# A transformer block with a mixture of experts: how token rows are scattered to their experts, when the expert stage begins, and which queue writes the output

## The chip, the core and the metric

The kernel runs on one core of a Trainium2 chip. A core has TensorE (PE, the matrix multiplier), VectorE (DVE), ScalarE (ACT), GpSimd (POOL), and SyncE (SP), which only issues transfers (DMAs). POOL and ACT can issue DMAs too, each on a queue of its own. [...] PSUM holds what PE writes, in eight banks; SBUF is the on-chip memory; DRAM is the memory outside.

The metric is the device time of one execution in microseconds (us). Before the change it is 938.62 us, the median of three runs (936.95 to 940.47).

## The reference

Input x is 8 sequences of 512 tokens of 256 values. A layer norm feeds two branches whose results are added to x:

```python
xn = layernorm(x)
# attention: 16 heads of 64, causal, keys and values through a latent of 128
latent = xn @ w_kv_down
k, v   = split(latent @ w_kv_up);  q = xn @ w_q
att    = softmax(causal(q @ k.T / 8))
attn   = (att @ v) @ w_out
# feed-forward: 8 experts of width 128, two for each token, and a shared one of width 256
scores = sigmoid(xn @ gate_w.T + lb_bias);  topw, topi = top_k(scores, 2)
topw   = topw / (topw.sum(-1) + 1e-8)
for e in range(8):
    m = topi == e
    wmean = (topw * m).sum() / max(m.sum(), 1)
    y = (silu(xn @ gw[e].T) * (xn @ uw[e].T)) @ dw[e].T
    out += where(m.any(-1), y * wmean, 0)
out += shared_mlp(xn)
return x + attn + out
```

There are 4096 tokens, so 8192 pairs of a token and one of its experts. How many go to one expert depends on the data.

## The kernel before

**Experts by sorted rows.** The kernel does not multiply every token by every expert. A DRAM buffer `xg_d` has 39 tiles of 256 slots (`NET`, line 88: 8192 / 256 plus seven for the experts' last, partly filled tiles). The router (line 309) works out a slot for each token and choice, with each expert starting at a tile boundary. `scatter_rows(n)` (line 442) writes the 128 normalised rows of token tile n to their slots by two indirect DMAs on POOL's queue, one for each choice, with a small memset after each. A row has 256 values and 16 more; one of these is the token's number. 39 x 256 slots less 8192 rows leaves 1792 slots empty. Before the scatters, `fill_zeros` (line 238, 13 calls) writes the whole buffer with rows of zeros that carry the number of a spare row.

For each tile t of the 39, `expert_fetch` gathers the expert's weights (POOL's queue) and loads the 256 rows (SP's queue); `expert_turn` transposes the rows on PE; `expert_hidden` and `expert_down` are the two layers; and `expert_add` adds the results, 128 rows at a time, to the token's row in `acc_d`, the DRAM accumulator (an indirect, adding DMA on POOL's queue; each waits for the one before to have landed). `acc_d` is started with x by `begin_sums` (SP), and each sequence's projected attention and shared result is added to it by `add_projection` (POOL). At the end `bring_out` copies seven sequences from `acc_d` to the output, DRAM to DRAM; the eighth goes by way of SBUF.

**Attention by pairs.** The loop over m (line 902) runs over 64 pairs of heads: pair m is heads 2p and 2p+1 of sequence b, m = 8b + p. In each pair PE makes scores, four strips of 128 queries (line 619); VectorE adds the mask and finds minima (626); ScalarE takes the exponentials (633); VectorE transposes blocks of 32 x 32 into `blk` (646); sixteen DMAs of 80 KB carry the blocks into their places, `pt<-blk` (`moved`, 658, called the moves here); and two pairs later PE multiplies by the values (`weighted`, 708). ScalarE copies that out and POOL multiplies it by the inverse sums (721), which come by way of DRAM (`row`, on POOL's queue, and `rb`, on SP's). `blk` and `pt` have two buffers each.

**The order of the work** is written out by hand. `put(m, place, f)` puts a piece of work into pair m at a place; the loop takes it in order of place, between scores and exponentials. The engines' order follows the order of the calls. Three stages differ:

- pairs 0 to 13: layer norms of the next sequences, layout of the experts' weights, zero fills, and in pairs 11 to 13 the router (mostly VectorE). Up to here POOL issues 5 of a pair's 16 moves, SP 11.
- pairs 14 to 21 (`S0` = 14 to `E0` = `BLOCK0` = 22): the scatters, four token tiles a pair, eight indirect DMAs on POOL's queue. `scattering` gives POOL 1 of the 16 moves, ScalarE 5 (issued by `rest`, after the exponentials of the pair's first half) and SP 10. Until `BLOCK0` a pair's strips go in two groups, (0, 3) and (1, 2), and the values' product comes late in the pair.
- pairs 22 to 63: all strips in one group, (3, 1, 2, 0), the product earlier in the pair, and the 39 experts spread evenly over half-pairs: expert t stands at half-pair `first + t * n_halves // NET` = 49 + 67 t // 39, its fetch four half-pairs ahead. From pair 59 (`END`) POOL and SP issue eight moves each.

Output projections of a sequence (lines 802 to 806) fall in the third and fourth pair of the sequence after it, so in pairs 10, 11, 18, 19, 26, 27 and so on; shared hidden chunks in the fifth and sixth. These pairs are long on PE; those with neither are short.

Of the kernel before, what the change touches and what calls it, by code (L numbers as in the profile page):

```python
# [33 lines left out]
F32 = mybir.dt.float32  # L34
I32 = mybir.dt.int32
AF = mybir.ActivationFunctionType
ALU = mybir.AluOpType
AX = mybir.AxisListType
# [3 lines left out]
P = 128  # L42
MASKED = 1.0e30
NO_MIN = 3.0e38
TOPK = 2
SLOTS = 256
# [3 lines left out]
def kernel(  # L50
# [17 lines left out]
    nc = tc.nc  # L68

    B, T, C = x.shape  # L70
# [6 lines left out]
    E = gate_w.shape[2]  # L77
    I = eg_w.shape[3]
    NS = sd_w.shape[1]
    NT = B * T  # L80
    NTILE = NT // P
    NQ = T // P
# [4 lines left out]
    QSCALE = -(float(D) ** -0.5)  # L87
    NET = NT * TOPK // SLOTS + E - 1
    NU = SLOTS // P

    const = ctx.enter_context(tc.tile_pool(name="const", bufs=1))
    wts = ctx.enter_context(tc.tile_pool(name="wts", bufs=1))
    keep = ctx.enter_context(tc.tile_pool(name="keep", bufs=1))
# [28 lines left out]
    outf = out.rearrange("b t c -> (b t) c")  # L122
# [10 lines left out]
    W = C + 16  # L133
    xnp, tmp_pools = ExitStack(), ExitStack()
    xns = xnp.enter_context(tc.tile_pool(name="xnp", bufs=1)).tile([P, NTILE, W], F32, name="xn")
# [3 lines left out]
    def load_x(b, first=0, count=NQ, by=nc.sync):  # L139
# [40 lines left out]
        out=mask[:, T - P :],  # L180
# [52 lines left out]
            wall_d[:, ds(at, n)].rearrange("(e p) i -> p e i", p=P)[:, es], w  # L233
        )

    NZ = 3

    def fill_zeros(k):
        nc.gpsimd.dma_start(
            xg_d[ts(k, NZ * SLOTS), :].rearrange("(n p) c -> p n c", p=P),  # L240
            zero.unsqueeze(1).broadcast_to([P, NZ * NU, W]),
        )

    def begin_sums(b):

        if b == B:
# [62 lines left out]
    def router():  # L309
# [67 lines left out]
        nc.vector.tensor_reduce(tiles, need, AX.X, ALU.add)  # L377
        end = rt.tile([P, E], F32, name="end")
        nc.vector.tensor_tensor_scan(end, ones[:, :E], tiles, 0.0, ALU.mult, ALU.add)
        yield  # L380

        upto = rt.tile([P, E, NTILE], F32, name="upto")
# [52 lines left out]

    between = keep.tile([P, 1], F32, name="between")
    at_i = keep.tile([P, TOPK, NTILE], I32, name="at_i")
    wrow_i = keep.tile([P, NET], I32, name="wrow_i")
    coef = keep.tile([P, NET], F32, name="coef")


    def scatter_rows(n):

        for k in range(TOPK):
            ins = nc.gpsimd.indirect_dma_start(  # L445
                out=xg_d[:, :],
                out_offset=bass.IndirectOffsetOnAxis(ap=at_i[:, k, n : n + 1], axis=0),
                in_=xns[:, n, :],
                in_offset=None,
            )  # L450
            tc.declare_no_dep(ins.ins, group="scatter", reason="rows of different slots")
            tc.add_to_no_dep_group("scatter", ins.ins)
            nc.gpsimd.memset(between, 0.0)

    def swiglu(g, u, th, h):

# [20 lines left out]

    def expert_fetch(t):

        w = ep.tile([P, WR], F32, bufs=4, name="w")  # L480
        nc.gpsimd.indirect_dma_start(
            out=w[:, :],
            out_offset=None,
            in_=wall_d[:, :],
            in_offset=bass.IndirectOffsetOnAxis(ap=wrow_i[:, t : t + 1], axis=0),
        )
        xg = ep.tile([P, NU, W], F32, bufs=3, name="xg")
        nc.sync.dma_start(xg, xg_d[ts(t, SLOTS), :].rearrange("(u p) c -> p u c", p=P))
        fetched[t] = w, xg

    def expert_turn(t):
        xg = fetched[t][1]

        pss = [bank([P, NU, NCC, D], "ps_x") for _ in range(2)]
        for u in range(NU):
            for cc in range(NCC):
                for j in range(2):
                    nc.tensor.transpose(  # L498
                        pss[j][:, u, cc, :], xg[ts(j, D), u, ts(cc, P)],
                        ident[ts(j, D), ts(j, D)],  # L500
                    )
        xgT = ep.tile([P, NCC, SLOTS], F32, bufs=2, name="xgT")
        for j in range(2):
            nc.scalar.copy(
                xgT.rearrange("p c (u j q) -> p j u c q", j=2, q=D)[:, j], pss[j]
            )
        to = ep.tile([P, NU], I32, bufs=4, name="to")
        nc.gpsimd.tensor_copy(to, xg[:, :, C].bitcast(I32))
        turned[t] = xgT, to

# [242 lines left out]
        )  # L753

    def bring_out(b):
        nc.sync.dma_start(outf[ts(b, T), :], acc_d[ts(b, T), :])

    def bring_back():
        nc.sync.dma_start(
# [6 lines left out]

    EARLY, HALF = 0.3, 0.65
    S0 = 14
    E0 = BLOCK0 = S0 + NTILE // NQ
    plan: dict = {}  # L770

    def put(m, place, f, *a):
        if place >= 2:
            m, place = m + 1, place - 2
        plan.setdefault(m, []).append((place, len(plan[m]) if m in plan else 0, f, a))
# [57 lines left out]
    def put_half(h, place, f, *a):  # L833
        put(h // 2, h % 2 + place, f, *a)
# [16 lines left out]
    LN_END = ((B - 2) * LNH // 2 + 6) // 2  # L851
    for k in range(4 * NCC + 2):
        put(1 + k, 0.45, lay_out_weights, k)
    for k in range(NET // NZ):
        put(k, 1.45, fill_zeros, k)
    for b in range(B + 1):
        put(NPAIR + 1 if b == 0 else E0 - B + b - 1, 0.55, begin_sums, b)

# [11 lines left out]
    for k in range(12):  # L870
        put(R0 + k // 4, 0.35 + 0.5 * (k % 4), lambda: next(steps, None))
    assert S0 == R0 + 3
    for n in range(NTILE):
        put(S0 + n // NQ, 0.35 + 0.5 * (n % NQ), scatter_rows, n)


    def begin_experts():
# [8 lines left out]
    first, n_halves = 2 * E0 + 5, 2 * (END - E0) - 7  # L886
    for t in range(NET):
        h = first + t * n_halves // NET
        put_half(h - 4, 0.5, expert_fetch, t)
        put(h // 2, -1, expert_turn, t)  # L890
        put(h // 2, (0.23, 0.67)[h % 2], expert_hidden, t)
        put_half(h + 1, 0.15, expert_down, t)
        for u in range(NU):
            put_half(h + 2 + u, 0.45, expert_add, t, u)
# [125 lines left out]
```

## Time and profile before

| what | value |
|---|---|
| median of three runs | 938.62 us |
| profiled execution, whole | 948.27 us |
| its span | 946.5 us |
| PE busy | 902.4 us (95%) |
| POOL busy | 598.9 us (63%) |
| VectorE busy | 579.8 us (61%) |
| ScalarE busy | 506.3 us (53%) |
| granted clock of PE, mean | 0.984 |
| DMA, all | 190.76 MB, mean 202 GB/s |
| scatters `xg_d<-xn,at_i` | 64, 979 ns each on POOL |
| zero fills `xg_d<-zero` | 13 of 816 KB, 920 ns each on POOL |
| additions `acc_d<-ye,to` | 78, 1635 ns each on POOL |

The profile is of one execution, and lists for each group of instructions its line, engine, operation and tiles ("out<-in"), its busy time, and the idle time before it with what ended that idle time. "SPq", "ACTq" and "POOLq" are the issues of transfers by these engines. Stages can be cut out and the engines' busy time summed for each, with the granted clock of PE (1.00 is full) and the mean busy share of the 16 DMA engines. A DMA's issue takes its engine's time, and its data land later.

### The profile page before, as it was taken

The numbers are of one execution on the slowest core, as the hardware profiler recorded it, in microseconds if no ns is written. First come the engines' busy times: TensorE is split into PE (matmuls) and PEld (weight loads), VectorE is DVE, ScalarE is ACT, GpSimd is POOL, SyncE is SP. The second block draws the span as 40 slices with busy tenths as digits, with TensorE's granted clock in tenths as the row PEclk, the third lists the DMA queues.
The fourth block names the chain that finished last, engine by engine and source line by source line (L and its number), as shares of the span: only waits on it lengthen the run. The fifth ranks groups of instructions, "written<-read, shape, count | busy, mean of one in ns | idle before, by whom it ended". The sixth has DMA issues, their size and how long they took to land. (4 is left out here: it accounts for less than half of the span.)

```text
span 946.5 us, 20282 instructions
## 1 busy us (share of the span) xinstructions
PE 902.4 (95%) x6380; PEld 475.8 (50%) x6380; DVE 579.8 (61%) x2041; ACT 506.3 (53%) x1506; POOL 598.9 (63%) x825
## 2 busy tenths in 40 slices
PE   8898999998789889999999999999999999999998
PEld 3354455533344345554555545565555654555546
DVE  3975764895534667446665466744677446674671
ACT  3654654445444467545665456744577445674550
POOL 2795883427776865647766666685668666766560
PEclk9999999999899989999999999999999999999999
DMA  7589888667886988768888778887778978886892
GB/s 275 155 256 261 263 247 295 154 165 222 219 232 172 255 224 220 181 150 202 193 205 190 167 180 195 214 185 185 165 194 188 211 180 189 192 184 149 203 271 76
DMA packets 127225, 190.76 MB, mean 202 GB/s; under 512 B 24688, under 2 KB 88432, under 8 KB 126880
## 3 DMA queue, kind: packets, MB, share of 16 engines
q1 hardware_dynamic: 87984, 107.73, 42.0%
q0 software_dynamic: 36656, 78.19, 34.9%
q10 hardware_dynamic: 2480, 3.55, 1.5%
q8 instruction: 52, 0.85, 0.4%
q14 instruction: 53, 0.43, 0.2%
HBM read 66.45 MB, written 50.05 MB: 123 GB/s over the span
## 5 line engine op out<-in xcount | busy, mean ns | idle before, releaser
L626 DVE CUSTOM_DVE_ANT_0 ps_s<-ps_s,mask 128x128 f32<-128x128 f32 (+3 forms) x512 | 238.9, 519 | 200.3 <-PE ps_s L619 160.1
L633 ACT ACTIVATE pr<-ps_s,mn 128x128 f32<-128x128 f32 (+3 forms) x512 | 268.3, 535 | 131.7 <-DVE mn L626 89.0
L646 DVE STREAM_TRANSPOSE blk<-pr 128x384 f32<-128x384 f32 (+2 forms) x512 | 206.5, 445 | 25.7 <-DMA pt<-blk 6.0
L540 POOL DMA_INDIRECT acc_d<-ye,to x78 | 127.5, 1635 | 116.7 <-DMA acc_d<-ye,to 44.2
L665 POOL DMA_DIRECT2D pt<-blk x303 | 164.9, 720 | 46.3 <-PE ps_q L117 15.6
L619 PE MATMUL ps_s<-k,q 64*128 64x128 f32 (+3 forms) x1024 | 168.8, 448 | 12.0 <-issue 5.7
L708 PE MATMUL ps_y<-pt,v 128*64 128x512 f32 (+3 forms) x1024 | 159.7, 456 | 11.8 <-DMA xnT_d<-lnT 3.9
L619 PEld LDWEIGHTS ps_s<-k,q 64*128 64x128 f32 x1024 | 92.0, 188 | 73.3 <-issue 38.8
L721 POOL TENSOR_TENSOR yT<-yT,rb 128x512 f32<-128x512 f32 x62 | 85.9, 1385 | 67.6 <-ACT yT L720 56.3
L117 PE MATMUL ps_o<-wo_sb,yT 128*64 128x256 f32 x1024 | 121.5, 379 | 2.7 <-issue 2.7
L117 PE MATMUL ps_q<-xnT,wq_sb 128*64 128x512 f32 x512 | 121.9, 597 | 0.0
L708 PEld LDWEIGHTS ps_y<-pt,v 128*64 128x64 f32 x1024 | 74.6, 142 | 93.8 <-issue 72.9
L633 ACT ACTIVATION_READ_ACCUMULATOR pr<-ps_s,mn 128x1 f32 x512 | 108.0, 211 | 0.0
L117 PEld LDWEIGHTS ps_o<-wo_sb,yT 128*64 128x64 f32 x1024 | 77.4, 137 | 37.4 <-issue 5.3
L117 PE MATMUL ps_e<-xgT,w 128*64 128x256 f32 x624 | 74.1, 379 | 0.8 <-DMA w<-wall_d,wrow_i 0.8
L626 DVE DVE_READ_ACCUMULATOR2_ANT mn<- 128x1 f32 x512 | 72.4, 141 | 0.0
L117 PEld LDWEIGHTS ps_q<-xnT,wq_sb 128*64 128x64 f32 x512 | 37.7, 139 | 67.6 <-issue 61.9
L117 PE MATMUL ps_v<-wkv_sb,lat 128*64 128x256 f32 x512 | 68.2, 387 | 2.9 <-ACT k L584 2.9
L445 POOL DMA_INDIRECT xg_d<-xn,at_i x64 | 62.7, 979 | 13.2 <-issue 13.2
L117 PE MATMUL ps_k<-lat,wkv_sb 128*64 128x512 f32 x256 | 69.4, 620 | 1.0 <-issue 1.0
L687 POOL DMA_DIRECT2D row<-riT x64 | 50.9, 796 | 17.0 <-DVE riT L685 14.4
L744 ACT COPY po<-ps_o 128x256 f32<-128x256 f32 x28 | 10.5, 374 | 95.3 <-PE ps_o L117 80.0
(131 smaller groups left out, 955.3 us busy)
## 6 DMA issues: line engine op xcount, KB each, us to landing
pt<-blk SPq DMA_DIRECT2D x681, 80.0 KB
pt<-blk POOLq DMA_DIRECT2D x303, 80.0 KB
rb<-row SPq DMA_DIRECT2D x128, 128.0 KB
xg_d<-zero POOLq DMA_DIRECT2D x13, 816.0 KB
xg<-xg_d SPq DMA_DIRECT2D x39, 272.0 KB
acc_d<-in_x_dram SPq DMA_DIRECT2D x8, 512.0 KB
xin<-in_x_dram SPq DMA_DIRECT2D x7, 512.0 KB
xnT_d<-lnT SPq DMA_DIRECT2D x7, 512.0 KB
```

What stands on the lines that cost most here:

```text
L117: nc.tensor.matmul(out[ts(j, D)], lhsT[:, ts(j, D)], rhs, start=start, stop=stop)
L445: ins = nc.gpsimd.indirect_dma_start(out=xg_d[:, :], out_offset=bass.IndirectOffsetOnAxis(ap=at_i[:, k, n : n + 1], axis=0), in_=xns[:, n, :],
L540: nc.gpsimd.indirect_dma_start(out=acc_d[:, :], out_offset=bass.IndirectOffsetOnAxis(ap=turned[t][1][:, u : u + 1], axis=0), in_=results[t ...
L619: nc.tensor.matmul(pss[j][:, ds(at, n)], q[ts(j, D), ts(i, P)], k[ts(j, D), :n], start=True, stop=True,)
L626: nc.vector.tensor_tensor_reduce(out=pss[j][:, ds(at, n)], in0=pss[j][:, ds(at, n)], in1=mask[:, T - n :], scale=1.0, scalar=NO_MIN, op0=A ...
L633: nc.scalar.activation(o, s, AF.Exp, bias=mn, scale=-1.0, accum_out=rs[:, j, i : i + 1])
L646: nc.vector.transpose(blk[:, :, j, i : i + (nr - 1) * (NQ - 1) + 1 : NQ - 1, :].rearrange("p b c q -> p c b q"), pr[:, j, : nr * P].rearra ...
L665: by.dma_start(pt[ts(kb, QB), a], blks[b, p][ts(a, QB), kb])
L687: nc.gpsimd.dma_start(row.rearrange("a x q -> (a x) q"), riT)
L708: nc.tensor.matmul(ps[ts(j, D), :, c:, :], vs[b, h // VH][:, c, ts(h % VH, D)], pts[b, p][:, :, j, at : at + NQ - c, :], start=(c == 0), s ...
L721: nc.gpsimd.tensor_tensor(y, y, rb, ALU.mult)
L744: nc.scalar.copy(pos[b][:, tt % 2, :], ps)
```

## The change

- **Scatters.** Three token tiles a pair in place of four (`SR` = 3), so the 32 tiles take eleven pairs, 14 to 24. `E0` and `BLOCK0` become 25: strips in two groups, POOL's single move and ScalarE's five last until pair 24, and the 39 experts are spread over the half-pairs from 55 on: 55 + 61 t // 39. `begin_sums` for sequences 1 to 7 and the spare rows, which counts back from `E0`, moves three pairs later.
- **Zeros.** The 13 fills of the whole buffer go. The router finds the 1792 empty slots (eight more VectorE instructions in the step that ends with `end`), and 14 indirect DMAs on POOL's queue scatter 128 rows of zeros each to them (`scatter_empty`): seven in pair 13, and one in each of pairs 14 to 20. `scatter` is the part of `scatter_rows` that both use.
- **Fetches** stand five half-pairs ahead of their expert, not four, with a buffer more for the weights (5), the rows (4) and the token numbers (5).
- **Outputs.** `bring_out` issues its copies from ScalarE's queue, not SP's.

```diff
+    NEMPTY = (NET * SLOTS - NT * TOPK) // P
...
-    NZ = 3
-
-    def fill_zeros(k):
-        nc.gpsimd.dma_start(
-            xg_d[ts(k, NZ * SLOTS), :].rearrange("(n p) c -> p n c", p=P),
-            zero.unsqueeze(1).broadcast_to([P, NZ * NU, W]),
-        )
...
+        none = rt.tile([P, E], F32, name="none")
+        nc.vector.scalar_tensor_tensor(
+            none, tiles, float(SLOTS), cnt, ALU.mult, ALU.subtract
+        )
+        ahead = rt.tile([P, E], F32, name="ahead")
+        nc.vector.tensor_tensor_scan(ahead, ones[:, :E], none, 0.0, ALU.mult, ALU.add)
+        nc.vector.tensor_tensor(ahead, ahead, none, ALU.subtract)
+        kth = rt.tile([P, NEMPTY], F32, name="kth")
+        nc.vector.tensor_scalar(kth, count[:, :NEMPTY], float(P), here, ALU.mult, ALU.add)
+        past = rt.tile([P, NEMPTY, E], F32, name="past")
+        nc.vector.tensor_tensor(
+            past, kth.unsqueeze(2).broadcast_to([P, NEMPTY, E]),
+            ahead.unsqueeze(1).broadcast_to([P, NEMPTY, E]), ALU.is_ge,
+        )
+        nc.vector.tensor_tensor(
+            past, past, cnt.unsqueeze(1).broadcast_to([P, NEMPTY, E]), ALU.mult
+        )
+        filled = rt.tile([P, NEMPTY], F32, name="filled")
+        nc.vector.tensor_reduce(filled, past, AX.X, ALU.add)
+        nc.vector.tensor_tensor(empty_i, kth, filled, ALU.add)
...
     def scatter_rows(n):
         for k in range(TOPK):
-            ins = nc.gpsimd.indirect_dma_start(
-            ...
-            nc.gpsimd.memset(between, 0.0)
+            scatter(at_i[:, k, n : n + 1], xns[:, n, :])
+
+    def scatter(at, rows):
+        ins = nc.gpsimd.indirect_dma_start(
+            out=xg_d[:, :],
+            out_offset=bass.IndirectOffsetOnAxis(ap=at, axis=0),
+            in_=rows,
+            in_offset=None,
+        )
+        tc.declare_no_dep(ins.ins, group="scatter", reason="rows of different slots")
+        tc.add_to_no_dep_group("scatter", ins.ins)
+        nc.gpsimd.memset(between, 0.0)
+
+    def scatter_empty(k):
+        scatter(empty_i[:, k : k + 1], zero)
...
-        w = ep.tile([P, WR], F32, bufs=4, name="w")
+        w = ep.tile([P, WR], F32, bufs=5, name="w")
...
-        xg = ep.tile([P, NU, W], F32, bufs=3, name="xg")
+        xg = ep.tile([P, NU, W], F32, bufs=4, name="xg")
...
-        to = ep.tile([P, NU], I32, bufs=4, name="to")
+        to = ep.tile([P, NU], I32, bufs=5, name="to")
...
     def bring_out(b):
-        nc.sync.dma_start(outf[ts(b, T), :], acc_d[ts(b, T), :])
+        nc.scalar.dma_start(outf[ts(b, T), :], acc_d[ts(b, T), :])
...
     S0 = 14
-    E0 = BLOCK0 = S0 + NTILE // NQ
+    SR = 3
+    E0 = BLOCK0 = S0 - (-NTILE // SR)
...
-    for k in range(NET // NZ):
-        put(k, 1.45, fill_zeros, k)
...
+    for k in range(NEMPTY):
+        n = NEMPTY // 2
+        put(S0 - 1 + max(k - n + 1, 0), 0.37 + (k < n) * 0.2 * k, scatter_empty, k)
     for n in range(NTILE):
-        put(S0 + n // NQ, 0.35 + 0.5 * (n % NQ), scatter_rows, n)
+        put(S0 + n // SR, 0.35 + (0, 0.5, 1)[n % SR], scatter_rows, n)
...
-        put_half(h - 4, 0.5, expert_fetch, t)
+        put_half(h - 5, 0.5, expert_fetch, t)
```

More of the change, by code (lines that the diff above doesn't have):

```diff
@@ L437 @@
     at_i = keep.tile([P, TOPK, NTILE], I32, name="at_i")
+    empty_i = keep.tile([P, NEMPTY], I32, name="empty_i")
     wrow_i = keep.tile([P, NET], I32, name="wrow_i")
@@ L444, in scatter_rows @@
         for k in range(TOPK):
[L445 to L452, printed above, removed]
-            nc.gpsimd.memset(between, 0.0)
+            scatter(at_i[:, k, n : n + 1], xns[:, n, :])
[11 more added lines that the diff above has]
+        scatter(empty_i[:, k : k + 1], zero)
     def swiglu(g, u, th, h):
```

## The prediction

> **What bounds the kernel now.** I read the busy shares first: TensorE (PE) is busy 902.4 of 946.5 us, the next engine 598.9. So the time is PE's work plus PE's stalls, and I looked for where the stalls lie. The timeline of PE near the end gives the price of an undisturbed pair. Columns: start, us, then the instruction; a bracket is idle time before it and what ended it.
>
> ```profile
> 888.78 2.43 PE L619 MATMUL ps_s<-k,q 64*128 64x512 f32 x16
> 891.14 2.38 PE L708 MATMUL ps_y<-pt,v 128*64 128x512 f32 x16
> ...
> 897.06 2.43 PE L619 MATMUL ps_s<-k,q 64*128 64x512 f32 x16
> ...
> 905.33 2.43 PE L619 MATMUL ps_s<-k,q 64*128 64x512 f32 x16
> 909.86 4.07 PE L708 MATMUL ps_y<-pt,v 128*64 128x512 f32 x16 [2.10 <-DMA out_dram<-acc_d]
> ```
>
> From one set of scores to the next an attention pair alone takes 897.06 - 888.78 = 8.28 us. By the same timeline a latent adds 1.7, a shared hidden chunk 3.4, half an output projection 8.6, a turn of normalised rows 0.6, the logits 1.9. What a pair takes beyond its own sum is stall. Next, the busy time of each engine in stages cut at the pairs' starts (PE, PEld, DVE, ACT, POOL, then granted clock, DMA share, GB/s):
>
> ```profile
> 71.80:142.00 70.20, 63.69 (x382) 32.51 (x380) 45.02 (x170) 38.49 (x113) 52.41 (x67) 0.95 0.89 257
> ...
> 204.50:218.10 13.60, 11.47 (x62) 4.66 (x60) 13.39 (x50) 6.22 (x20) 3.79 (x6) 1.00 0.34 82
> 218.10:261.50 43.40, 33.89 (x158) 13.95 (x156) 22.44 (x86) 21.67 (x69) 35.19 (x61) 0.88 0.85 239
> ...
> 283.00:324.10 41.10, 41.10 (x270) 18.92 (x268) 24.03 (x85) 18.22 (x55) 30.04 (x49) 1.00 0.74 205
> 324.10:352.10 28.00, 22.48 (x121) 10.52 (x121) 18.60 (x66) 16.46 (x51) 20.09 (x34) 0.88 0.81 222
> 352.10:880.50 528.40, 523.26 (x4079) 289.61 (x4075) 319.31 (x1102) 305.37 (x907) 345.35 (x423) 1.00 0.81 188
> ```
>
> The expert stage (last line, pairs 24 to 59) idles 5.1 us in 528: PE sets it. The stalls are before it: pairs 5 to 9 (first line), pair 14 (VectorE full: 13.39 of 13.60), pairs 15 to 17 (third), pairs 22 and 23 (fifth). Pairs 19 to 21 scatter too, yet PE is full there, because projection and shared work cover the scatters. In pairs 15 to 17 PE's timeline starts at
>
> ```profile
> 229.80 0.68 PE L619 MATMUL ps_s<-k,q 64*128 64x128 f32 x4
> ...
> 245.19 0.49 PE L619 MATMUL ps_s<-k,q 64*128 64x128 f32 x4
> ...
> 257.18 4.40 PE L708 MATMUL ps_y<-pt,v 128*64 128x512 f32 x16
> 261.52 1.35 PE L619 MATMUL ps_s<-k,q 64*128 64x128 f32 x8
> ```
>
> so pairs 16 and 17 take 15.4 and 16.3 us for 8.28 of work (pair 15: 218.10 to 229.80, 11.7). Two queues are full there. POOL's timeline runs one cycle of eight scatters in 13.5 us, 227.75 to 241.27, with a scatter every 1.3:
>
> ```profile
> 227.75 0.57 POOL L665 DMA_DIRECT2D pt<-blk  x1
> ...
> 229.21 1.01 POOL L445 DMA_INDIRECT xg_d<-xn,at_i  x1 [0.30 <-issue]
> ...
> 230.53 0.99 POOL L445 DMA_INDIRECT xg_d<-xn,at_i  x1 [0.19 <-issue]
> ...
> 241.27 0.56 POOL L665 DMA_DIRECT2D pt<-blk  x1 [0.76 <-issue]
> ```
>
> And ScalarE stops its exponentials to issue its own moves (three here, five a pair):
>
> ```profile
> 230.39 1.90 ACTq L665 DMA_DIRECT2D pt<-blk  x3
> 232.34 0.47 ACT L633 ACTIVATE pr<-ps_s,mn 128x256 f32<-128x256 f32 x1 [2.39 <-DMA pt<-blk]
> ```
>
> Last, SP's timeline: eleven moves cost 12.52 us of issue in pair 4-5, 7.22 late in the expert stage; two output copies cost 2.19.
>
> ```profile
> 69.54 12.52 SPq L665 DMA_DIRECT2D pt<-blk  x11
> ...
> 847.48 7.22 SPq L665 DMA_DIRECT2D pt<-blk  x11
> ...
> 895.23 2.19 SPq L756 DMA_DIRECT2D out_dram<-acc_d  x2
> ```
>
> **The change, part by part.** I sum against the profiled execution (948.27, span 946.5) and put the difference on the median of 938.62; the profiled run is 1% longer than the median, which on a difference of ten is 0.1 us.
>
> A. *Zero fills gone.* Thirteen DMAs of 816 KB, 10.6 MB, leave POOL's queue, with 13 x 0.92 = 12.0 us of POOL. Six fall in 71.8 to 142: 4.9 of 70.2 x 257 = 18.0 MB, 27%. The DMA share of 0.89 would fall to some 0.65, below the 0.81 at which eleven moves take 7.22 to issue. Stalls beyond their own sums: pair 5, 20.71 us against 8.28 + 3.4 + 1.3 + 1.9 = 14.9, so 5.8; pair 8, 14.99 against 11.5, so 3.5; pair 6, 0.8. Both large ones end when late pt moves land. Bounds: 0 (the delay is the order on SP's queue) to -10. I take -6, nearest to the bandwidth row. In its place 14 scatters of 128 rows x 1088 B = 1.9 MB; seven go in pair 13, where POOL is idle 5.89 us before one instruction and 5.36 before the next: 7 x 1.3 = 9.1 fits. Without that cover 9.1 us would delay pair 14's move, which has a whole pair before it is read.
>
> B. *Finding the empty slots.* Eight more VectorE instructions in pair 12. Rows: five small ones like L391 (171 ns), three like L372 and L377 (291 and 286): 1.7 us. VectorE is full by pair 14, so I put +1.5 on the path (0 to 1.7).
>
> C. *Three tiles a pair over eleven pairs.* Pairs 14 to 20 carry seven scatters, 21 to 23 six, 24 four. The cycle of 13.5 becomes 12.2, 10.9 and 8.3. (i) Pairs 15 to 17 last 43.4 now; one scatter less should give 1.3 each, and pair 18, 4.6 over its sum from the lag, some 1. Here a rule weighs in. The last PE line but one above shows 16 matmuls in 4.40 us against 2.38: PE ran at half clock, 0.88 granted on the mean, though no idle gap here is over 2.5 us. The Trainium skill ("TensorE: Matmul & The Clock Gate", Part 1) has the clock fall after an idle window of about 3.4 us; by it these stalls would cost only their idle, 9.5 us. The row has 43.4 - 3 x 8.28 = 18.6. By the rule (i) is worth half, -2.5; by the row -5. I take the row (0 to -9). (ii) Pairs 22 to 24 become scatter pairs with two groups, and the experts' PE work they held moves later, unchanged. Their own sums are 10.0, 8.28, 8.28. Cheap end: as pairs 19 to 21, 0.4 each, 1.2. Dear end: as pairs 15 to 17, 6.2 each, 18.6. They are short, like the dear ones, but have fewer scatters: cycles of 10.9, 10.9 and 8.3 with ScalarE's five issues (about 3.2 us) on top of its 7 us of work, so about 12, 11.5, 11: +8. (iii) The handover now costs pair 22 7.1 us (17.07 against 10.0) and pair 23 2.4 (10.96 against 8.5). At 324.10 POOL still has six scatters to issue, the last at 332.8, and PE waits 2.52 us for the first rows. With four scatters in the last pair that lag is mostly gone; fetches stand five half-pairs ahead, and a pair with 8.6 us of projection comes before the first expert: 9.5 falls to 3, -6.5 (-9.5 to -2). Late next is pt of the last scatter pair. SP's accumulator starts move three pairs later, still one pair ahead of the projections that add to them. C is -5 + 8 - 6.5 = -3.5.
>
> D. *Experts closer together, fetched sooner.* 39 experts in 61 half-pairs, not 67: 1.28 a pair, not 1.16. PE's sum is the same. POOL pays per expert 1.3 + 0.4 + 2 x 1.9 = 5.5, and 4.4 a pair; per four short pairs it loses 1 to 4 us of slack, covered by the long pairs after. I give +2.5 (0 to +8). The half-pair of lead removes PE's wait of 2.10 us for rows in pair 32: -2.1. The extra buffers keep reuse distances as they were. D is +0.5.
>
> E. *Outputs on ScalarE's queue.* The line at 909.86 waits 2.10 and then runs 4.07 for 2.38: 3.8 us, with SP's moves late by two copies. The Trainium skill ("Trainium Kernel Development and Optimization", Key Constraints) says all queues feed the same 16 DMA engines, so that another queue saves issue time alone: by it 2.2 comes back, by the row up to 3.8. I take 3. ScalarE pays 0.63 a copy, two a pair in 60 and 61: 1.3 against about 1.5 us that it waits there for the first minimum of each pair; uncovered, 2.6. The first copy also waits for the last expert's addition; behind it stand the projections' copies and the next exponentials. That addition was issued at 867.58, five us before ScalarE gets there. +0.5. E is -2.5.
>
> Sum: -6 + 1.5 - 3.5 + 0.5 - 2.5 = -10.0, so 938.6 - 10.0 = 928.6.
>
> **Rivals.** (1) *ScalarE's own moves pace the scatter pairs.* For it: its 2.2 to 4.3 us gaps in each of pairs 15 to 17; against: POOL's cycle is as long as the pair. Then one scatter less gives nothing and pairs 22 to 24 cost 6.2 each: C = 0 + 18.6 - 6.5 = +12, total -6 + 1.5 + 12 + 0.5 - 2.5 = +5.5, 944. It turns the sign when C passes +6.5, that is at 4.3 us a pair. (2) *The zero fills were hidden anyway*: SP waits for VectorE's blocks 120.9 us in all, so late moves may be late blocks. A = 0, 934.6: hardly to be told from no change. (3) *The change does not do what it says*: the order of instructions has the 14 new scatters in place and no fill, so only a repeated stall remains possible.
>
> **How the numbers follow.** My case 0.67, with its own range 920 to 934; rival 1 0.17; rival 2 0.14; others 0.02. Leaving 0.1 at each side takes the range to 919 and to rival 1's 944. A measurement of this kernel tells 0.5% (4.7 us; its three runs span 3.5). Below 933.9: 0.61 from my case and 0.06 from rival 2. Above 943.3: most of rival 1 beyond its own middle and the tail, 0.15. The rest, 0.18.
>
> **What would show it.** A: pairs 5 and 8 near 15 and 11.5 us, eleven moves near 7 us of issue. C: pairs 15 to 17 near 13, pairs 22 to 24 near 11 to 12 with POOL's cycles about 11; rival 1 shows 14 or more with ScalarE's gaps unchanged. Handover: no wait of PE for xg. D: stalls in the short pairs if POOL falls behind. E: no wait at the ps_y of the last pair, or new gaps of ScalarE before exponentials. I am wrong if the three added scatter pairs cost over 4 us each, or if the early stalls stay.

## The result, and the profile after

The changed kernel takes 956.27 us (median of 8 runs, 945.77 to 966.2) against 939.1 for the kernel before beside it (8 runs, 936.95 to 941.59): 1.0137 times, interval 1.0099 to 1.0174. It is slower by about 13 us, where 928.6 was predicted with a range of 919 to 944. (Three of its eight runs, 964 to 966 us, were in a slower state; the ratio leaves them out, and so gives 13 us where the medians differ by 17.) Its profiled execution has a span of 955.8 us.

The page after, engines and clock:

```profile
span 955.8 us, 20311 instructions
...
PE 912.2 (95%) x6380; PEld 482.3 (50%) x6380; DVE 579.3 (61%) x2049; ACT 505.0 (53%) x1506; POOL 595.8 (62%) x828
...
PEclk9899999989999989999999999999998999999999
```

PE has the same work, yet is busy 912.2 us, not 902.4, and idle 955.8 - 912.2 = 43.6 us against 44.1 before. The added time is in the busy column: matmuls that run at half speed after a stall. A view of idle time alone would not have shown it.

The stages of the changed kernel, cut at the starts of pairs (window, length, then PE, PEld, DVE, ACT, POOL busy, granted clock, DMA share, GB/s). The rows shown are pairs 5 to 9, 14, 15 to 17, 22 and 23, 24 and 25, 27 to 38, and 39 to 50:

```profile
72.00:131.70 59.70, 59.70 (x382) 30.48 (x380) 44.72 (x170) 37.66 (x110) 45.49 (x60) 1.00 0.81 223
194.30:210.60 16.30, 14.11 (x64) 5.65 (x61) 14.18 (x54) 6.67 (x21) 13.39 (x22) 0.79 0.62 180
210.60:242.00 31.40, 29.51 (x160) 12.61 (x158) 22.33 (x84) 18.97 (x61) 27.43 (x48) 0.95 0.77 236
...
303.80:326.30 22.50, 20.62 (x116) 8.79 (x114) 14.95 (x56) 13.06 (x41) 17.08 (x30) 1.00 0.84 255
326.30:351.20 24.90, 21.21 (x106) 9.76 (x104) 17.01 (x60) 15.11 (x50) 17.23 (x28) 0.86 0.81 234
369.50:553.60 184.10, 182.91 (x1432) 101.09 (x1428) 109.31 (x374) 104.75 (x311) 108.21 (x131) 1.00 0.77 180
553.60:753.50 199.90, 185.18 (x1416) 106.04 (x1412) 108.64 (x372) 105.95 (x314) 129.14 (x153) 0.97 0.77 182
```

Pairs 5 to 9 last 59.7 us, not 70.2; pairs 15 to 17 last 31.4, not 43.4. Both gains are there. They are lost mainly in pairs 39 to 50: 14.7 us idle in 199.9, at a clock of 0.97, where the expert stage before idled 5.1 in 528 at 1.00.

To compare kernels I take each pair's length less the sum of its own PE instructions, each at the pace that it has in undisturbed pairs. What is left is the pair's stall, idle and slowed work together; an undisturbed pair of the expert stage leaves 0.31. The kernel before and the changed one were profiled again beside two experiments, on one chip (stalls in us):

```
pairs      before   changed   half the adds   outputs by SyncE
0-10        23.8     14.4        14.8             15.2
11-14        6.9      9.3         7.9              8.0
15-21       19.1     12.1        15.2             14.1
22-26       14.1     18.4        18.4             17.5
27-58       16.7     39.8        10.1             41.1
59-63        6.9      9.4        10.0              6.5
span       939.7    954.8       928.2            954.0
```

The expert stage, pairs 27 to 58, gives away 23.1 us. Everything else together gains 7.2 (the sums leave 0.8 of the spans' 15.1 us unaccounted for).

In the first trace the stalls of that stage lie in pairs 39 to 41, 46, 48, 50 and 57, all short ones or, like 50, next to them. POOL's timeline of the changed kernel in pairs 46 to 50 (start, us, instruction, idle time before it and what ended that):

```profile
687.28 1.62 POOL L562 DMA_INDIRECT acc_d<-ye,to  x1 [2.16 <-DMA acc_d<-ye,to]
692.92 1.56 POOL L562 DMA_INDIRECT acc_d<-ye,to  x1 [4.03 <-issue]
...
696.40 2.53 POOL L687 DMA_DIRECT2D pt<-blk  x5
699.23 1.69 POOL L562 DMA_INDIRECT acc_d<-ye,to  x1 [0.30 <-issue]
...
704.72 1.64 POOL L562 DMA_INDIRECT acc_d<-ye,to  x1 [0.92 <-POOL yT L743]
...
710.75 1.67 POOL L562 DMA_INDIRECT acc_d<-ye,to  x1 [1.25 <-DMA acc_d<-ye,to]
...
716.84 1.62 POOL L562 DMA_INDIRECT acc_d<-ye,to  x1 [1.66 <-issue]
...
723.22 1.70 POOL L562 DMA_INDIRECT acc_d<-ye,to  x1 [0.30 <-issue]
730.02 1.59 POOL L562 DMA_INDIRECT acc_d<-ye,to  x1 [5.11 <-ACT ye L555]
```

Each addition starts 5.5 to 6.8 us after the one before it, and POOL's five moves of 696.40 stand behind the addition at 692.92, which waited 4.03 us. PE and ScalarE in the same stretch:

```profile
701.61 4.07 PE L730 MATMUL ps_y<-pt,v 128*64 128x512 f32 x16 [3.75 <-DMA pt<-blk]
...
730.05 2.93 PE L641 MATMUL ps_s<-k,q 64*128 64x256 f32 x10 [4.57 <-ACT ye L555]
```

```profile
729.31 0.69 ACT L555 ACTIVATE ye<-ps_ed,coef 128x512 f32<-128x512 f32 x1 [6.04 <-DMA acc_d<-ye,to]
```

Two kinds of stall come from one chain. At 701.61 PE has waited for moves that POOL issued late. At 729.31 ScalarE has waited 6.04 us for a result buffer `ye`, which the chain of additions still held; PE waited 4.57 us for ScalarE. The list of waits of the changed kernel (us in all, times, longest; "issue" is a wait for which the profile shows no cause):

```profile
POOL acc_d L562 <- issue: 49.2, 38, 5.2
POOL acc_d L562 <- DMA acc_d<-ye,to: 47.9, 20, 5.2
...
POOL acc_d L562 <- ACT ye L555: 24.7, 6, 5.1
...
ACT ye L555 <- DMA acc_d<-ye,to: 19.8, 5, 6.0
```

The line of 24.7 us looks as if POOL waited for ScalarE's results, but it is the chain too. The addition at 730.02 is for the experts' tile 26 (of 39, from 0), whose result had been written by 707.5; what ScalarE finished at 730.00 was the result of tile 28. The landing of the addition of 723.22 released both engines. All six waits of that line are of this kind: the addition's own result was at least 12 us old.

In the kernel before, ScalarE's wait at that instruction is for PE, and for the additions only once, while POOL's additions already wait for one another:

```profile
POOL acc_d L540 <- DMA acc_d<-ye,to: 44.2, 20, 5.0
POOL acc_d L540 <- issue: 43.2, 42, 4.8
...
ACT ye L533 <- PE ps_ed L117: 9.3, 12, 2.0
...
ACT ye L533 <- DMA acc_d<-ye,to: 0.5, 1, 0.5
```

### The profile page after: what moved, and what is told of

Same layout as the page of the kernel before. It is cut to its first block, busy times and chain, and to the rows that moved or that the text cites. A ratio compares the mean times of both kernels' runs of the same rounds, so it can differ in the third digit from the quotient of the medians.

```text
span 955.8 us, 20311 instructions
## 1 busy us (share of the span) xinstructions
PE 912.2 (95%) x6380; PEld 482.3 (50%) x6380; DVE 579.3 (61%) x2049; ACT 505.0 (53%) x1506; POOL 595.8 (62%) x828
## 5 line engine op out<-in xcount | busy, mean ns | idle before, releaser
L562 POOL DMA_INDIRECT acc_d<-ye,to x78 | 127.2, 1630 | 135.9 <-issue 49.2
L641 PE MATMUL ps_s<-k,q 64*128 64x128 f32 (+3 forms) x1024 | 179.1, 457 | 19.9 <-ACT ye L555 9.3
L687 POOL DMA_DIRECT2D pt<-blk x291 | 156.8, 680 | 55.5 <-DVE riT L707 30.3
L641 PEld LDWEIGHTS ps_s<-k,q 64*128 64x128 f32 x1024 | 95.7, 190 | 85.0 <-issue 32.6
L730 PEld LDWEIGHTS ps_y<-pt,v 128*64 128x64 f32 x1024 | 75.7, 142 | 95.6 <-issue 70.2
L118 PEld LDWEIGHTS ps_e<-xgT,w 128*64 128x64 f32 x624 | 46.1, 137 | 29.7 <-issue 11.3
```

The costliest lines, as they stand in the source:

```text
L118: nc.tensor.matmul(out[ts(j, D)], lhsT[:, ts(j, D)], rhs, start=start, stop=stop)
L562: nc.gpsimd.indirect_dma_start(out=acc_d[:, :], out_offset=bass.IndirectOffsetOnAxis(ap=turned[t][1][:, u : u + 1], axis=0), in_=results[t ...
L641: nc.tensor.matmul(pss[j][:, ds(at, n)], q[ts(j, D), ts(i, P)], k[ts(j, D), :n], start=True, stop=True,)
L687: by.dma_start(pt[ts(kb, QB), a], blks[b, p][ts(a, QB), kb])
L730: nc.tensor.matmul(ps[ts(j, D), :, c:, :], vs[b, h // VH][:, c, ts(h % VH, D)], pts[b, p][:, :, j, at : at + NQ - c, :], start=(c == 0), s ...
```

## The experiments

Medians of the kernel before differed between the five groups of runs that follow (953.7, 939.1, 949.7, 936.8 and 936.4), and on one and the same chip too (949.7 and 936.8), although the texts on record speak of a slower chip. So each ratio is to the kernel before of its own group, on its own chip.

### One part at a time

Only the zero rows scattered to the empty slots, all else as before. Against the changed kernel:

```diff
-    SR = 3
+    SR = 4
...
-        put_half(h - 5, 0.5, expert_fetch, t)
+        put_half(h - 4, 0.5, expert_fetch, t)
...
-        nc.scalar.dma_start(outf[ts(b, T), :], acc_d[ts(b, T), :])
+        nc.sync.dma_start(outf[ts(b, T), :], acc_d[ts(b, T), :])
```

(with the buffers of before, and the scatters at 0.35 + 0.5 n as before)

> The kernel before with the zeros' part alone: no fills, 14 scatters of zero rows, the eight VectorE instructions; scatters four tiles a pair, experts from pair 22, fetches four half-pairs ahead, outputs by SP. Theory 1 (the loss is in the closer experts: the additions to the accumulator, each of which waits for the one before to land, fall behind in short pairs) expects the relief of pairs 5 to 9 seen after the change, some 10 us, less 1 to 2 for VectorE, and an expert stage as before: 929 us (926 to 934). Theory 2 (the loss is in fetching sooner) expects the same. If the zero rows' scatters themselves did harm, 939 or more.

> The kernel before with the zeros' part alone (the same as x1_zeros_only, which had 0.996 on another chip). Pairs 5 to 10 save 8 us, VectorE's eight instructions take 1 to 2.5 back, the expert stage is as before: a ratio of 0.993 (0.989 to 0.997).

Measured: 947.35 us, 0.9959 [0.9929, 0.9989], and in the other group 932.41 us, 0.9947 [0.9923, 0.9971]. This part alone is a gain of half a per cent, and of the versions that compute the whole output it is the only one that is faster than the kernel before.

Only the experts closer together, on the kernel before:

```diff
-    first, n_halves = 2 * E0 + 5, 2 * (END - E0) - 7
+    first, n_halves = 2 * E0 + 11, 2 * (END - E0) - 13
```

> The kernel before with one thing changed: the 39 experts are spread from half-pair 55 over 61 half-pairs, as after the change, in place of 49 and 67. Scatters, fills, fetches, blocks and outputs as before. Theory 1 expects all of the expert stage's loss here: in the changed kernel pairs 27 to 58 lost 24 us against before, and pairs 22 to 26 here only get emptier, so about 960 us (950 to 970), with waits of some 5 us for additions in short pairs. Theory 2 expects 937 to 943.

> The kernel before with the experts alone moved: from half-pair 55 over 61 half-pairs (the same as x2_late_experts), now beside a trace of the kernel before from the same chip. If the closer spacing alone makes the loss, pairs 27 to 58 have 15 to 25 us more stalls than in that trace, and the ratio is 1.01 to 1.025. If the spacing needs the sooner fetches or the outputs to do harm, pairs 27 to 58 differ by less than 8 us and the ratio is under 1.008.

> The kernel before, for its trace on this chip. A ratio of 1.00.

Measured: 960.98 us, 1.0101 [1.002, 1.0181]; again 944.23 us, 1.0088 [1.0053, 1.0123], where the kernel before, run as one of the kernels, came to 1.0036 [0.9999, 1.0073]. In that second group pairs 27 to 58 stall 26.5 us, against 16.7 in the kernel before. Closer experts alone cost 8 to 10 us, with every other edit left out.

Only the sooner fetches (with their larger buffers), and only the outputs on ScalarE's queue, each on top of the zero rows:

```diff
-        put_half(h - 4, 0.5, expert_fetch, t)
+        put_half(h - 5, 0.5, expert_fetch, t)
```

> The kernel before with the zero rows scattered to the empty slots alone, and with the fetches five half-pairs ahead and their larger buffers; the experts stand where they stood, the output goes by SyncE. Theory S (the closer experts alone make the chain of additions fall behind): as the zero rows alone, 0.995 of the kernel before, and pairs 27 to 58 stall about 13 us. Theory F (sooner fetches crowd the queues and cost by themselves): over 1.003, with pairs 27 to 58 at 20 us or more.

```diff
-        nc.sync.dma_start(outf[ts(b, T), :], acc_d[ts(b, T), :])
+        nc.scalar.dma_start(outf[ts(b, T), :], acc_d[ts(b, T), :])
```

> The kernel before with the zero rows scattered to the empty slots alone, and with the seven output copies on ScalarE's queue; fetches and experts as before. Theory S: pairs 27 to 58 stall about 13 us as with the zero rows alone, and the copies cost only in pairs 59 to 63, 2 to 3 us: 0.997 to 0.998 of the kernel before. Rival (a copy on ScalarE's queue costs nothing by itself, and what was seen at the end came from late experts): 0.995, SyncE's eight moves near 6 us each in pairs 60 to 62. Theory O (the copies cost more than that): over 1.0.

Measured: 938.43 us, 1.0003 [0.9968, 1.0039], with 19.6 us in pairs 27 to 58; and 936.39 us, 0.9995 [0.9967, 1.0023], with 12.3 us there. Both points lie above what the theory of closer experts alone foretold. The sooner fetches' interval leaves 0.995 out, but 1.003 in: they appear to take back the gain of the zero rows, in a part of the same stage (19.6 us in place of the 13.2 of the zero rows alone). The intervals of the zero rows alone were taken in other groups, so the half per cent that each seems to cost is the less certain for it. For the copies 0.997 and 0.998 lie inside the interval, and the place foretold is seen: SyncE's eight moves, pairs 60 to 62, with the copies on ScalarE's queue,

```profile
872.87 8.17 SPq L687 DMA_DIRECT2D pt<-blk  x8
...
882.90 9.12 SPq L687 DMA_DIRECT2D pt<-blk  x8
...
893.79 7.14 SPq L687 DMA_DIRECT2D pt<-blk  x8
```

and with the zero rows alone, where SyncE issues the copies after them:

```profile
877.96 5.60 SPq L687 DMA_DIRECT2D pt<-blk  x8
883.60 1.92 SPq L778 DMA_DIRECT2D out_dram<-acc_d  x2
...
887.29 5.86 SPq L687 DMA_DIRECT2D pt<-blk  x8
...
896.21 5.76 SPq L687 DMA_DIRECT2D pt<-blk  x8
```

So the rival that a copy on ScalarE's queue costs nothing by itself falls. Late experts do a part of the same, though: with the spacing alone, and the copies on SyncE's queue, the first two of these groups of moves take 7.79 and 7.28 us.

### One part undone

The changed kernel and the kernel before once more, unedited:

> The changed kernel itself, beside the kernel before on the same chip, because the times of one kernel differed by 1.5% between two chips (before: 939 and 954 us). All theories expect the ratio found first, 1.014, within 0.8% either way; by stages, pairs 5 to 9 and 15 to 18 better than before by some 20 us and pairs 27 to 58 worse by some 20 to 25.

> The kernel before, for a trace of it on the chip of these runs. A ratio of 1.00. If the chip is one of the slower ones, its scatter stage and its short pairs of the expert stage show more stalls than the first trace (25 us in pairs 15 to 18, 16 us in pairs 27 to 58).

Measured: 958.47 us, 1.0168 [1.0074, 1.0263]; and 0.9993 [0.9968, 1.0018]. The table above is from these.

Fetches four half-pairs ahead with the buffers of before; five `ye` buffers, not three; outputs by SyncE; four token tiles a pair:

```diff
-        put_half(h - 5, 0.5, expert_fetch, t)
+        put_half(h - 4, 0.5, expert_fetch, t)
```

> The changed kernel with the fetches undone: four half-pairs ahead and the buffers of before (4, 3, 4). Theory 1 expects it to stay slow, 950 to 960 us. Theory 2 (a gather and a load of rows that stand sooner in POOL's and SP's queues delay the moves and sums behind them) expects the loss of the expert stage gone: 930 us (926 to 936).

```diff
-        y = ep.tile([P, NU, C], F32, bufs=3, name="ye")
+        y = ep.tile([P, NU, C], F32, bufs=5, name="ye")
```

> The changed kernel with five buffers, not three, for the experts' results, so that ScalarE need not wait for an addition to land before it writes the next. Theory 1 in its narrow form (late additions stop ScalarE by the result's buffer) expects ScalarE's 20 us of such waits gone and 940 us (935 to 947). Theory 1 in its wide form (POOL itself is late, and with it the sums' rows and the moves that SP holds behind them) expects a small gain, 950 to 955. Theory 2 expects no change.

```diff
-        nc.scalar.dma_start(outf[ts(b, T), :], acc_d[ts(b, T), :])
+        nc.sync.dma_start(outf[ts(b, T), :], acc_d[ts(b, T), :])
```

> The changed kernel with the outputs on SP's queue as before. If the outputs' part helps as predicted, this is 2 to 4 us slower than the changed kernel, in pair 63; if ScalarE's issues cost more than they free, it is 1 to 4 us faster, in pairs 59 to 62. Theories 1 and 2 expect pairs 27 to 58 as in the changed kernel.

```diff
-    SR = 3
+    SR = 4
```

> The changed kernel with four token tiles a pair, so scatters in pairs 14 to 21, two groups until pair 21 and the experts from half-pair 49 over 67 half-pairs, as before; zeros, fetches and outputs as changed. Theory 1 expects the expert stage as in the kernel before (some 16 us of stalls in pairs 27 to 58, not 40) and the scatter stage as before, so about 930 us, a ratio of 0.99 to the kernel before. If the sooner fetches or the outputs do the harm, it stays at 1.01.

Measured: 971.16 us, 1.015 [1.0076, 1.0224]; 982.62 us, 1.0329 [1.0243, 1.0414]; 954.64 us, 1.0171 [1.0105, 1.0237]; 961.6 us, 1.0136 [1.0067, 1.0205]. None of the four brings the time back. The stalls of pairs 27 to 58 are 35.6, 37.9, 41.1 and 20.8 us.

Three things follow. More result buffers do not help, so the short supply of buffers is a symptom: ScalarE's waits for the additions are gone there, but POOL's waits of one addition for another are 64.6 us in 25 places. Both forms of theory 1 expected less than 956 us of that run; why it is the slowest of all is not shown, as its group has no run of the changed kernel itself. The outputs by SyncE mend the end (6.5 us in pairs 59 to 63, against 9.4) and nothing else; the ratio, 1.0171 beside 1.0168, does not show it. And the wider spacing, which comes back with four tiles a pair, halves the stalls of the expert stage without giving back the time; in that run pairs 15 to 21 stalled 43.6 us, against 12.1 in the changed kernel of the table. That group has no profile of the kernel before, so how much of those 43.6 us is the edit and how much the occasion is not known. The occasion can do much: the kernel with the closer experts alone stalled 27.3 us in pairs 15 to 18 in the first of its two groups and 16.4 in the second.

### The additions

Half of them: the second 128 rows of each expert's tile are not added, so 39 of the 78 additions are left out.

```diff
-        for u in range(NU):
+        for u in range(NU - 1):
             put_half(h + 2 + u, 0.45, expert_add, t, u)
```

> The changed kernel without the second addition of each expert (39 of 78 are left out, so the output lacks half of the experts' rows). Theory 1 (the additions fall behind in short pairs) expects the stalls of pairs 27 to 58 to shrink to the steady 0.3 us a pair, some 10 us in all in place of 40, and a ratio to before near 0.98. If something else of the closer experts sets the stalls (bytes of weights and rows, SP's order), pairs 27 to 58 keep 25 us or more and the ratio stays over 1.00.

Measured: 928.36 us, 0.9898 [0.987, 0.9926], beside the changed kernel's 1.0168. Pairs 27 to 58 stall 10.1 us, the floor: 32 undisturbed pairs at 0.31 make 9.9. ScalarE's waits for the additions are gone from the list; its only long wait at that instruction is for PE:

```profile
ACT ye L555 <- PE ps_ed L118: 15.3, 19, 2.0
...
POOL acc_d L562 <- DMA acc_d<-ye,to: 1.6, 1, 1.6
```

This doesn't yet tell POOL's issue time, 39 x 1.63 = 64 us less, or bytes from the waiting of one addition for the next. So: all 78 are issued, the first half of each tile to one accumulator and the second to another. The second sum is not joined to the output.

```diff
+    acc2_d = dram.tile([NT_ALL, C], F32, name="acc2_d")
...
-            out=acc_d[:, :],
+            out=(acc_d, acc2_d)[u][:, :],
```

> The changed kernel with two accumulators: the second addition of each expert goes to one of its own (started like the first, by as many copies more in pairs 9 to 24), so that an addition waits for the landing of the one two before it, not of the one just before. All 78 additions are issued. (The second accumulator is not added to the output, which lacks those rows.) Theory 1a (the serial landing of the additions holds POOL) expects the stalls of pairs 27 to 58 to fall from 40 us to 10 to 15, as with half of the additions. Theory 1b (POOL's time for issuing 78 additions, or their bytes) expects 30 us or more to stay. The copies cost a few us in pairs 14 to 25 under both.

Measured: 957.42 us, 1.0105 [1.0066, 1.0143] (with the kernel before at 949.74). Pairs 27 to 58 stall 10.1 us again, and additions start as little as 1.91 us after one another, where the changed kernel's quickest is 4.1. The same additions with the same bytes, but half the chain: the stall goes. So it is the order of the additions, each behind the landing of the last, and not POOL's issue time nor the bytes. The time as a whole stays above the kernel before; in this run too pairs 15 to 18 stalled, by 30.8 us.

The waits of that run at the same places:

```profile
POOL acc_d L565 <- issue: 13.5, 52, 0.3
...
ACT ye L558 <- PE ps_ed L118: 12.7, 16, 2.0
...
POOL acc_d L565 <- DMA acc_d<-ye,to: 5.9, 6, 2.6
```

The waits without a cause in the profile fell with the others, from 49.2 us, the longest 5.2, to 13.5, the longest 0.3. So most of them were waits for a landing too.

Whole, with the second sum started from zeros in pairs 2 to 9, joined at the end by eight adding DMAs from DRAM to DRAM on POOL's queue, and outputs by SyncE:

```diff
+    def join_sums(b):
+        nc.gpsimd.dma_start(
+            acc_d[ts(b, T), :].rearrange("(n p) c -> p n c", p=P),
+            acc2_d[ts(b, T), :].rearrange("(n p) c -> p n c", p=P), accum_op=ALU.add,
+        )
```

> The changed kernel with two accumulators, complete: the second is started with zeros in pairs 2 to 9, takes the second addition of each expert, and is added to the first by eight DMAs on POOL's queue before the outputs, which are on SP's queue again and half a pair later. The serial landing as cause expects no stalls over the steady ones in pairs 27 to 58 (10 us, from 40), against 2 to 6 us more in the early pairs and at the end: a ratio to before of 0.985 to 1.00, and at least 15 us below the changed kernel's 1.014 to 1.017.

Measured: 948.55 us, 1.0133 [1.0104, 1.0163]. Pairs 27 to 58 are at 10.1 us once more (16.7 in the kernel before of that group), but pair 63 alone stalls 19.7 us, against 5.6, since POOL's moves of the last pairs wait for the joining DMAs:

```profile
POOL pt L701 <- DMA acc_d<-acc_d: 19.6, 5, 5.1
```

In this trace the gain was given back at the end. It is the quickest of the six runs, though (943.05 us), and its span is only 4.0 us over that of the kernel before in its group; where the other runs lose the rest of the 12 us is not shown. To let additions on one accumulator run without order was not tried, as two of them may meet on one row.

Wider spacing by a later end: the experts spread as far as pair 61, not 59, with the output copies and the even division of the moves starting there too, with three and with four token tiles a pair (the latter with the edit of `SR` shown above):

```diff
-    END = len(pairs) - 5
+    END = len(pairs) - 3
```

> The changed kernel with the experts' end two pairs later (END = 61): from half-pair 55 over 65 half-pairs, 1.20 experts a pair in place of 1.28, outputs two pairs later. Theory 1 expects most of the loss to go: 12 to 20 us of stalls in pairs 27 to 60, and about 935 us, ratio 0.99 to 1.00; some may come back in the last pairs, where the outputs are now issued. If spacing isn't the cause, 1.01 to 1.02.

> Both: four token tiles a pair and the experts' end two pairs later, so 39 experts from half-pair 49 over 71 half-pairs, 1.10 a pair, fewer than in the kernel before. Theory 1 expects no stalls over the steady 0.3 us in pairs 27 to 58 (10 us in all) and the best time of all, about 925 us, ratio 0.985, if the outputs' later place gives back no more than 3 us.

Measured: 970.45 us, 1.0228 [1.0182, 1.0274], and 953.78 us, 1.0058 [1.002, 1.0097]. In pairs 27 to 58 the stalls fall to 18.1 and 11.1 us, as a chain with more room should do. Neither kernel is faster: pairs 15 to 18 stall 27.2 and 32.8 us in these runs, and with four tiles the last pair 11.4. As fixes both fail; as a reading of the expert stage they agree.

## Why the prediction was wrong, step by step

The steps summed to -10; on one chip the stalls differ by +15.9. Of the 26 us between, D is 22.6 and E 5.0; A gave 3.4 more than it was priced at, and B and C were right to within 1 us. Rival 3, that the change does not do what it says, falls: its edits are all in the trace.

**A, the zero fills (-6): right, and on the small side.** Pairs 5 and 8 last 14.94 and 11.51 us, as foretold (15 and 11.5). In the first two traces pairs 0 to 10 lose 10.2 us of stall; beside one another on one chip, 9.4. The row that was followed, the DMA share, fell from 0.89 to 0.81, not to 0.65: the bytes of the stretch fell from 18.0 to 13.3 MB (223 GB/s x 59.7 us), as reckoned, but they now pass in a shorter time. Eleven moves of SyncE from pair 4 to pair 9 take 7.2 to 10.7 us:

```profile
64.90 10.66 SPq L687 DMA_DIRECT2D pt<-blk  x11
...
115.64 7.20 SPq L687 DMA_DIRECT2D pt<-blk  x11
```

It was enough. Alone, with B, it brings 0.4 to 0.5% of the time. Rival 2 (the fills were hidden) falls.

**B, VectorE (+1.5): right.** Pairs 11 to 14 add 2.4 us on one chip, nearly all in pair 14. In the first trace PE's wait there for ScalarE, which waits for VectorE's minima behind the router, is 2.19 us in place of 0.91, and a half-speed stretch follows (granted clock 0.79 in that pair, 1.00 before).

**C, three tiles a pair (-3.5): about right as a sum, wrong in its terms.** On one chip pairs 15 to 21 gain 7.0 and pairs 22 to 26 lose 4.3: -2.7. (i) is -7.0 for -5; pairs 16 and 17 last 9.3 and 10.0 us in the first trace, better than the 13 foretold. (ii) is right: pairs 22 to 24 stall 7.6 us, for 8. Rival 1, which wanted 6.2 a pair, falls as the general case. (iii) is wrong: the stall at the handover did not shrink from 9.5 to 3 but moved with it. Pairs 25 and 26 stall 8.6 us, and the working had looked only at POOL's lag. The trace at 336 us shows PE and ScalarE:

```profile
335.87 2.84 ACTq L687 DMA_DIRECT2D pt<-blk  x3
...
336.39 1.13 PE L641 MATMUL ps_s<-k,q 64*128 64x512 f32 x4
...
338.81 0.47 ACT L655 ACTIVATE pr<-ps_s,mn 128x256 f32<-128x256 f32 x1 [5.48 <-DMA pt<-blk]
...
339.43 3.57 PE L641 MATMUL ps_s<-k,q 64*128 64x256 f32 x12 [1.91 <-ACT pr L655]
```

In pair 25 scores need a bank that ScalarE has to read first. ScalarE has spent the 5.48 us before that on the moves of pair 23: it waited to issue them, and then issued the last three in 2.84 us. This is the mechanism of rival 1, in one pair. PE waits 1.91 us and then runs its next 12 matmuls at 297 ns each, where all 16 of an undisturbed pair, the four widest among them, take 2.43 us, 152 ns each. The wait for rows that was to vanish did vanish. This cause is read from the trace; no run tested it by itself.

**D, experts closer together (+0.5, at most +8): the step that failed.** On one chip it is +23.1 us. The prediction named the cost, POOL falling behind in short pairs, but sized it by POOL's time to issue: two additions of 1.9 us in an expert's 5.5, 4.4 a pair, "1 to 4 us of slack, covered by the long pairs after". What has to fit is not the issue but the chain. In the changed kernel a quarter of the additions start within 5.02 us of the one before (5.06 in the kernel before), and the quickest after 4.1. I take 5 us for a link that waits for nothing but the last landing. At 1.28 experts and two additions each that is 2.56 x 5.02 = 12.9 us a pair, over the 10.9 to 12.7 us that the short pairs have of PE's work; before, 2.33 x 5.06 = 11.8. This is an estimate from these rows, and it shows a chain near its limit, not by how much it is over: with the quickest link both sums, 10.5 and 9.7, would fit. The profile before the change said so too: POOL's waits of one addition for another are its 44.2 us in 20 places, shown above. They were read as slack of an engine that is busy 63%. A chain of landings is a resource of its own, which no engine's busy share shows.

What hangs on it: POOL's moves and its `row` behind an addition, SyncE's `rb` behind `row`, and a `ye` buffer for ScalarE. The long pairs cover no stall that PE has already had. Half the additions, and two chains, both bring this stage to its floor, and that is shown. That closer spacing loads the chain is shown too, by the spacing alone: +9.8 us in this stage, 1.0088 of the time. The rest of the 23.1 us is not settled. Put on by themselves, the zero rows take 3.5 us from this stage (13.2 for 16.7), the closer spacing adds 9.8 and the sooner fetches 6.4 (19.6 for 13.2): 12.7 in all, so about 10 us come only with the parts together. Taken away from the changed kernel (39.8), the fetches leave 35.6 and the closer spacing 20.8, though that run as a whole was no faster. So the spacing is the largest part both ways. That all the parts load the same chain fits these numbers; which share is whose no run tells, and each figure is from one trace, some of them from different groups.

**E, outputs on ScalarE's queue (-2.5): wrong in sign.** On one chip the end costs 9.4 us against 6.9 before, and 6.5 with SyncE's queue. One trace would not be enough for this, as the first trace of the kernel before has 9.2 there; but over all traces whose end differs in nothing else the end costs 5.7 to 9.2 us with SyncE's queue and 9.2 to 11.9 with ScalarE's. The rule of the Trainium skill that I weighed ("Trainium Kernel Development and Optimization", Key Constraints), that all queues feed the same DMA engines and another queue saves only issue time, was the nearer reading, and even it promised a gain of 2.2. SyncE's moves in the second trace of the changed kernel:

```profile
897.60 8.19 SPq L687 DMA_DIRECT2D pt<-blk  x8
...
907.57 8.00 SPq L687 DMA_DIRECT2D pt<-blk  x8
```

In the kernel before beside it:

```profile
884.92 5.79 SPq L665 DMA_DIRECT2D pt<-blk  x8
890.75 1.87 SPq L756 DMA_DIRECT2D out_dram<-acc_d  x2
...
894.40 6.91 SPq L665 DMA_DIRECT2D pt<-blk  x8
```

Two copies, 1.9 us together, left SyncE's queue, and its eight moves grew by 2.4 and 1.1 us, as the copies now run beside them and not after. Then the moves came later, not sooner: PE's last products wait 1.87 and 1.76 us for `rb`, in one of them

```profile
909.53 2.38 PE L730 MATMUL ps_y<-pt,v 128*64 128x512 f32 x16 [1.87 <-DMA rb<-row]
```

The stall of 3.8 us that was to be removed was also not a steady one: in the second trace of the kernel before the wait is 1.18 us with no slowed work behind it.

**The half clock.** The choice of the row over the rule of "TensorE: Matmul & The Clock Gate" (Part 1) held again: pairs 39 to 50 idle 14.7 us and stall 27.4, of which twelve undisturbed pairs would have 3.7, so an idle microsecond cost 1.6. The gaps here reach 4.57 us, where the rule allows it too. The one in pair 25, of 1.91 us, it does not: PE runs at a granted clock of 1.00 up to that gap, and at 0.50 from 340.13 us, 0.7 after it, to 346.96.

## What to carry to other kernels

Before work is packed closer, look for chains of DMAs that wait for one another's landing, and price them by start to start (5 us here), not by the engine's time to issue (1.6 us). A list of releasers that shows an instruction waiting for its own kind, 44 us in all, is the sign of it, however idle the engine. And a copy moved to another queue runs beside what it used to follow: ask whom it then slows.

## What the runs showed of the hardware

In this kernel, where each waits for the landing of the last, indirect adding DMAs of 128 rows on one tensor start 4.1 us after one another at the quickest and a quarter of them within 5.0; on two tensors in turn the quickest is 1.9 us. Eight moves of 80 KB on SyncE's queue in pairs 60 to 62 take 5.6 to 5.9 us to issue where the copies come after them and 7.1 to 9.1 where ScalarE's queue has the DRAM-to-DRAM copies (two traces of one group each; over all fast traces whose end is otherwise the same, 5.5 to 7.8 and 7.1 to 9.6). And the stage of the scatters differs from one occasion to the next by about as much as the change moved it (12.6 and 7.0 us less in two traces): pairs 15 to 18 of the kernel before stalled 25.1, 17.1 and 14.6 us in three traces, and 25.9 to 37.8 in seven kernels of the two groups in which the kernel before took about 950 us, whatever the edit. What sets it is open.
